# Layer 1's row sums: the product with ones one step later, in the bank of the product with v, and the division another step later

## The chip, the core and the metric

One core of one Trainium2 chip. The metric is the device time of one execution, in microseconds. The kernel before took 2955.73 us, the median of three runs (2946.95 to 2957.67).

## The reference, cut to what matters

Two cross-attention layers follow each other, on x of 4 batches x 1024 rows x 512 and a context of 4 x 1024 x 384, all in float32. Layer 0 has 16 heads of 64. Layer 1, in which the change lies, has 16 heads of 32 and works on layer 0's output:

```python
xn = x * jax.lax.rsqrt(jnp.mean(x * x, axis=-1, keepdims=True) + EPS_RMS) * norm_w
q = (xn @ wq).reshape(B, T_dec, N_HEADS, HEAD_DIM)
kv = (encoder_out @ wkv).reshape(B, T_enc, 2, N_HEADS, HEAD_DIM)
k, v = (kv[:, :, 0], kv[:, :, 1])
q = _rotate(q, cos, sin)
k = _rotate(k, cos, sin)
...
logits = jnp.einsum('bqhd,bkhd->bhqk', q, k) * scale
attn = jax.nn.softmax(logits, axis=-1)
out = jnp.einsum('bhqk,bkhd->bqhd', attn, v).reshape(B, T_dec, D_Q)
return residual + out @ wout
```

The line left out divides each head's q and k by their norms. Since they have norm 1, the exponentials of the logits need no maximum taken off. What the change touches is the division of the softmax: the sum of the exponentials over the keys of each query, and the division of the product with v by it.

## The kernel before, in words

The batches follow each other, and within one layer 0 comes before layer 1. Every engine works through its instructions in the order in which the code records them; nothing reorders them (manual_schedule). What one engine needs of another is a semaphore wait that the tile framework derives from the tiles that an instruction reads and writes.

Layer 1 of a batch is Attention1 (L555). It has two halves of eight heads each, a half has eight blocks, one for each of four query blocks qb (WQ = 256 queries) and each of two head groups g (four heads of 32 rows). A block has four steps, kk = 0 to 3, each of two key blocks of 128 keys, so there are 32 steps in a half, 64 in a batch and 256 in all, and 64 blocks. `step` (L570) records, in this order:

- 8 matmuls of the scores (L577; the profile counts each float32 matmul as two, so 16 there) into two PSUM tiles s of two banks each, and two exponentials from them on ScalarE (L587), into e.
- `finish` (L599): the division that was left over from the step before, if any, and then `product` (L607), the 8 matmuls (L616) of the exponentials of the step before with v, which add up in av[:, 0] over the four steps of a block.
- The filler (L591): `Units.fill` takes off a queue of units as many as their noted costs allow. They are projections (L163), transposes, and output products, with all that hangs on them on the other engines: the rotation of q and k on VectorE (L476 to L483), the norms, the adds of output products to x (L293). In the first half of a batch they make q, k and v of the layer, in the second half output products and the next batch's preparation. In the last half of the last batch there are only output products, which are added to the queue at given steps n (L873 to L876), once the o that they read has been recorded.
- On VectorE, the sum of the two key blocks' exponentials, two adds (L593) into both[:, kk], and in steps 1 and 2 an add of that to both[:, 0] (L597). After a block, both[:, 0] and both[:, 3] together hold the exponentials summed over the eight key blocks.

What is left is the sum over the 128 partitions. `product` does it after the last step of a block (L623): 8 matmuls with a matrix of ones (L627), of both[:, 0] and both[:, 3], into av[:, 1]. These stand right after the last product with v, that is in step 0 of the next block. ScalarE then copies both halves of av to avs (L631), and one step later VectorE takes the reciprocal of the sums in avs (L634) and multiplies (L635) into o.

Each block takes a new av tile, from PSUM's slot f0, which has one buffer; the filler's banks (`bank`, L126) are f1 to f3 during layer 1, and f0 to f3 otherwise. The tile `both` is four slots of 4 x 256 columns.

Of the kernel before, what the change touches and what calls it, by code (L numbers as in the profile page):

```python
# [31 lines left out]
F32 = mybir.dt.float32  # L32
# [4 lines left out]
P = 128  # L37
S = 1024
NT = S // P
# [8 lines left out]
HD1 = 32  # L48
# [60 lines left out]
def xattn_kernel(ctx: ExitStack, tc: tile.TileContext, a: dict, out: bass.AP):  # L109
    nc = tc.nc  # L110
# [6 lines left out]
    ps_f = ctx.enter_context(tc.tile_pool(name="ps_f", bufs=1, space=bass.MemoryType.PSUM))  # L117
    ctx.enter_context(tc.manual_schedule())

    def score(name, shape=(P, S)):  # L120
        return ps_s.tile(list(shape), F32, tag="s", name=name)
# [18 lines left out]
    ones = const.tile([P, HD1], F32, name="ones")  # L140
# [211 lines left out]
    class Attention0:  # L352


        def __init__(self, b, units):
            self.b, self.u = b, units
            self.blocks = deque()
            self.turn = self.raw = None
# [194 lines left out]
    WQ = 256  # L553

    class Attention1:  # L555


        def __init__(self, b, units):
            self.b, self.u = b, units
            self.last = None  # L560
            self.av = None
            self.quotient = None
            self.e = sb.tile([P, 2, 2, 2, 2, WQ], F32, tag="e", bufs=2, name=f"e1_{b}")
            self.both = sb.tile([P, 4, 4, WQ], F32, tag="big", bufs=2, name=f"both_{b}")
            rest = sb.tile([P, 4, 1024], F32, tag="big", bufs=2, name=f"rest_{b}")
            self.avs = rest[:, 0].rearrange("p (n c q) -> p n c q", n=2, c=2)
            v1 = rest[:, 2:].rearrange("p g (t f) -> p g t f", f=P)
            self.v1 = [v1[:, g] for g in range(2)]

        def step(self, half, g, qb, kk, kT, qT, v, o, us):  # L570
            n = f"{self.b}_{half}_{g}_{qb}_{kk}"
            sc = [score(f"s1_{n}_{u}", (P, 2, 2, WQ)) for u in range(2)]
            for c in range(2):
                for j in range(4):
                    rr = slice(j * HD1, (j + 1) * HD1)
                    k = 2 * kk + c
                    nc.tensor.matmul(  # L577
                        sc[j // 2][:, j % 2, c, :],
                        kT[rr, g, k * P : (k + 1) * P],
                        qT[rr, g, qb * WQ : (qb + 1) * WQ],  # L580
                        start=True,
                        stop=True,
                    )
            es = []
            for u in range(2):
                e = self.e[:, kk % 2, u]
                nc.scalar.activation(e, sc[u], AF.Exp, scale=float(np.sqrt(np.float32(HD1))))  # L587
                es.append(e)
            self.finish()
            self.last = (half, g, qb, kk, v, es, o)  # L590
            self.u.fill(us)  # L591
            for u in range(2):
                nc.vector.tensor_add(  # L593
                    self.both[:, kk, 2 * u : 2 * u + 2, :], es[u][:, :, 0, :], es[u][:, :, 1, :]
                )
            if 0 < kk < NT // 2 - 1:
                nc.vector.tensor_add(self.both[:, 0], self.both[:, 0], self.both[:, kk])  # L597

        def finish(self):  # L599

            if self.quotient is not None:
                self.quotient()
                self.quotient = None
            if self.last is not None:
                self.product()

        def product(self):  # L607
            half, g, qb, kk, v, es, o = self.last
            n = f"{self.b}_{half}_{g}_{qb}"
            if kk == 0:  # L610
                self.av = ps_f.tile([P, 2, WQ], F32, tag="f0", name=f"av1_{n}")
            first, end = kk == 0, kk == NT // 2 - 1
            for c in range(2):
                for j in range(4):
                    rr = slice(j * HD1, (j + 1) * HD1)
                    nc.tensor.matmul(  # L616
                        self.av[rr, 0, :],
                        v[g][:, 2 * kk + c, rr],
                        es[j // 2][:, j % 2, c, :],
                        start=first and c == 0,  # L620
                        stop=end and c == 1,
                    )
            if end:  # L623
                for i in (0, NT // 2 - 1):
                    for j in range(4):
                        rr = slice(j * HD1, (j + 1) * HD1)
                        nc.tensor.matmul(  # L627
                            self.av[rr, 1, :], ones, self.both[:, i, j], start=i == 0, stop=i > 0
                        )
                s = self.avs[:, qb % 2]  # L630
                nc.scalar.copy(s, self.av)  # L631

                def divide():
                    nc.vector.reciprocal(s[:, 1, :], s[:, 1, :])  # L634
                    nc.vector.tensor_mul(o[g][:, qb * WQ : (qb + 1) * WQ], s[:, 0, :], s[:, 1, :])  # L635

                self.quotient = divide
            self.last = None


# [5 lines left out]
    def flat(lists):  # L646
        return [u for lst in lists for u in lst]
# [52 lines left out]
    work = Units()  # L700
# [15 lines left out]
    for b in range(B):  # L716
# [7 lines left out]
        for p in range(NPAIR):  # L724
# [8 lines left out]
            elif p % 2 == 0:  # L733
                i = p // 2 - 1
# [4 lines left out]
                    lambda n, i=i: wo[i][:, n % 2, :],  # L739
# [14 lines left out]
            if p == NPAIR - 1:  # L754
# [7 lines left out]
                v = []  # L762
# [10 lines left out]
            n = 7 * (p == 0)  # L773
# [10 lines left out]
            for i in range(NT):  # L784
# [8 lines left out]
                n = NT * (NPAIR - p) - i  # L793
# [27 lines left out]
        att1 = Attention1(b, work)  # L821
        o = [
            sb.tile([P, S], F32, tag="vals", bufs=4, name=f"o1_{b}_{g}") if g < 2 else None
            for g in range(4)
        ]
# [6 lines left out]
        for half in range(2):  # L832
            n = 0
            if half == 0:
                vs = value_chains(att1.v1, wv1, ct, f"pv1_{b}_1")
                first = [q[1], (norms[1]["stats"], [], []), vs[0], (norms[1]["apply"], [], k1[1][2]), k1[2]]
                rest = [(norms[1]["turn"] + q[2][0], [], q[2][2]), k1[3], q[3], q1[0], vs[1], q1[1], q1[2]]
                rest += [q1[3], vs[2], vs[3]]
                chains = first + rest
                work.add(weave(chains, 2))  # L840
                def mark(c):

                    i = chains.index(c)
                    return sum(len(x[0]) for x in chains[: i + 3]) + sum(len(x[2]) for x in chains[: i + 1])

                base = work.done
                marks = {8: base + mark(q[1]), 16: base + mark(rest[0]), 24: base + mark(q[3])}
            else:
                for g in range(2, 4):
                    o[g] = sb.tile([P, S], F32, tag="vals", bufs=4, name=f"o1_{b}_{g}")  # L850
                wo1 = [wo_load(a["wout"], i, f"wo1_{b}_{i}") for i in range(2)]
                adds = add_units(xt, lambda n: o[n], lambda n: wo1[0][:, n % 2, :], f"po1_{b}_0", (0, 1))
                if b + 1 < B:
                    st, order = prepare_units(b + 1)
                    first, later = order(adds)
                    work.add(first)
                else:
                    work.add(flat(adds))
            blocks = [(qb, g) for qb in range(S // WQ) for g in range(2)]
            final = b == B - 1 and half == 1  # L860
            if final:
                blocks.sort(key=lambda block: block[1])
                adds = [
                    add_units(
                        xt, lambda n: o[n], lambda n: wo1[1][:, n % 2, :], f"po1_{b}_{i}", (i,), store if i == 3 else None
                    )
                    for i in (2, 3)
                ]
            for qb, g in blocks:
                for kk in range(NT // 2):  # L870
                    if half == 0 and n in marks:
                        work.until(marks[n])
                    if final and n == 18:  # L873
                        work.add(flat(adds[0]))
                    if final and n in (22, 26, 30):
                        work.add(flat(adds[1][(n - 22) // 2 : (n - 18) // 2]))  # L876
                    att1.step(half, g, qb, kk, kT, qT, v, o[2 * half :], work.total() / (32 - n))
                    n += 1
            work.drain()
            kT, qT, v = kT1, qT1, att1.v1  # L880
        att1.finish()
        att1.quotient()
        which["from"], which["cols"] = 0, 2
        if b == B - 1:
            tail = flat(adds[1][6:])
        else:
            outs = add_units(
                xt, lambda n, o=o: o[n], lambda n, w=wo1[1]: w[:, n % 2, :], f"po1_{b}_1", (2, 3), store
# [40 lines left out]
```

## Time and profile before

| | |
|---|---|
| runs, median (lowest, highest) | 2955.73 us (2946.95, 2957.67) |
| profiled execution: its own time | 2957.42 us |
| profiled execution: span of the instructions | 2955.4 us |
| granted TensorE clock, mean | 0.992 |
| TensorE, VectorE, ScalarE busy | 2865.9, 2185.6, 1436.6 us |
| TensorE idle within a first half of layer 1 | 6.1 us of 128 to 130 us |
| TensorE idle within a second half, batches 0 to 2 | 0.3 us of 123 us |
| L627, product with ones | 1024 in the profile (512 in the code), 81.3 us busy |
| L634, reciprocal | 64, mean 1748 ns |
| L635, multiplication | 64, mean 498 ns |
| L631, copy of av | 64, mean 587 ns |

The page gives busy times by engine, the chain of work that ended last, and groups of instructions with the idle time ahead of them. The answers on waits give, for each pair of instruction and releaser, the idle time in total, how often, and the longest. In the timeline each line is a run of like instructions: start, duration, engine, line, operation, tiles, and in brackets the idle time of the engine ahead of it with what ended it. The rows by window give, after the length, the busy time of PE, PEld, DVE, ACT and POOL with instruction counts, then the granted TensorE clock (PEclk) as a share of full speed, the share of DMA and GB/s. PE is TensorE (PEld its weight loads), DVE VectorE, ACT ScalarE, POOL GpSimd, SP SyncE.

### The profile page before, as it was taken

What the parts mean: (1) busy time and instruction counts of PE and PEld (TensorE: products, weight loads), DVE (VectorE), ACT (ScalarE), POOL (GpSimd) and SP (SyncE); (2) the same over time, 40 slices, a digit from 0 to 9 for tenths busy, and PEclk for the clock granted to TensorE, in tenths of its full rate; (3) what the DMA queues carried; (4) which work ended last, traced back from release to release, by engine and by line L of the source; (5) the groups of instructions that cost most, each with busy time, mean ns of one, the idle gap of its engine ahead of it and who ended that gap; (6) DMA issues with size and microseconds to landing.
All of it is one profiled execution on the core that took longest, in us unless ns stands there. A gap on an engine that the chain in (4) does not pass through costs nothing.

```text
span 2955.4 us, 66614 instructions
## 1 busy us (share of the span) xinstructions
PE 2865.9 (97%) x27336; PEld 1433.0 (48%) x27336; DVE 2185.6 (74%) x2952; ACT 1436.6 (49%) x2265; POOL 935.9 (32%) x776
## 2 busy tenths in 40 slices
PE   8999999999989999999998999999999999999998
PEld 4444445555444454555544444455554444445544
DVE  5677785877767778587776777868877677786787
ACT  4444444656434443466643444346664344444664
POOL 2343353320234335332023433534102343353310
PEclk9999999999999999999999999999999999999999
DMA  5878774010487877401048787730105887763000
GB/s 141 197 180 188 169 173 104 22 36 25 105 199 176 186 163 164 104 22 36 25 115 189 179 187 170 162 94 22 36 25 126 192 182 178 172 162 85 2 2 30
DMA packets 177552, 348.86 MB, mean 118 GB/s; under 512 B 37600, under 2 KB 93152, under 8 KB 177248
## 3 DMA queue, kind: packets, MB, share of 16 engines
q1 hardware_dynamic: 175920, 343.96, 49.5%
q8 instruction: 215, 3.52, 0.5%
q14 instruction: 89, 0.73, 0.1%
q10 hardware_dynamic: 1328, 0.66, 0.1%
HBM read 67.64 MB, written 8.39 MB: 26 GB/s over the span
## 4 chain that ended last, share of the span: by engine, by line
PE 80%; DVE 10%; SPq 4%; DMA 2%; issue 2%; ACT 1%; POOL 1%; DVEq 0%; ACTq 0%
PE s L365 15%; PE av L426 13%; PE po L163 10%; PE s L577 8%; PE pqT L163 7%; PE pv L163 7%; PE av L616 6%; PE pkT L163 6%; SPq L410 4%; PE q_p L163 3%; PE av L627 2%; DVE both L593 2%; DVE m L390 2%; PE k_p L163 1%; DMA wo<-in_Wo_dram 1%
## 5 line engine op out<-in xcount | busy, mean ns | idle before, releaser
L390 DVE TENSOR_REDUCE m<-s 128x1 f32<-128x1024 f32 x512 | 603.0, 1220 | 401.6 <-PE s L365 401.6
L587 ACT ACTIVATE e<-s 128x1024 f32<-128x1024 f32 x512 | 497.1, 1023 | 313.2 <-PE s L577 304.7
L391 ACT ACTIVATE e<-s,m 128x1024 f32<-128x1024 f32 x256 | 283.4, 1112 | 502.9 <-DVE m L390 240.7
L396 POOL TENSOR_SCALAR raw<-raw,li 128x1024 f32<-128x1024 f32 x256 | 286.4, 1119 | 734.2 <-DVE li L395 725.8
L365 PE MATMUL s<-qk 64*128 64x512 f32 x2048 | 518.1, 621 | 0.7 <-ACT qk L135 0.7
L391 ACT ACTIVATE raw<-s,m 128x1024 f32<-128x1024 f32 x256 | 285.9, 1117 | 470.0 <-DVE m L390 470.0
L426 PE MATMUL av<-eT,v 128*64 128x256 f32 x4096 | 470.4, 382 | 5.3 <-DMA eT<-e 2.3
L396 POOL TENSOR_SCALAR e<-e,li 128x1024 f32<-128x1024 f32 x256 | 286.3, 1119 | 493.8 <-DMA eT<-e 239.4
L593 DVE TENSOR_TENSOR both<-e 128x512 f32<-128x512 f32 x512 | 341.9, 701 | 116.1 <-ACT e L587 88.9
L426 PEld LDWEIGHTS av<-eT,v 128*64 128x64 f32 x4096 | 287.4, 137 | 225.2 <-issue 84.5
L365 PEld LDWEIGHTS s<-qk 64*128 64x128 f32 x2048 | 180.9, 188 | 283.9 <-issue 174.3
L577 PE MATMUL s<-q,k 32*128 32x256 f32 x4096 | 306.0, 401 | 5.9 <-ACT q L504 2.7
L399 DVE STREAM_TRANSPOSE e<-e 128x1024 f32<-128x1024 f32 x256 | 310.1, 1229 | 0.2
L399 DVE STREAM_TRANSPOSE e<-raw 128x1024 f32<-128x1024 f32 x256 | 310.0, 1229 | 0.0
L163 PE MATMUL po<-wo,vals 128*64 128x512 f32 x1024 | 242.7, 608 | 26.5 <-DMA wo<-in_Wo_dram 26.5
L577 PEld LDWEIGHTS s<-q,k 32*128 32x128 f32 x4096 | 192.2, 184 | 153.0 <-ACT e L587 72.1
L163 PE MATMUL pqT<-hT,w 128*64 128x512 f32 (+1 forms) x1216 | 240.7, 595 | 2.5 <-ACT hT L247 2.5
L293 DVE TENSOR_TENSOR x<-x,po 128x512 f32<-128x512 f32 x200 | 131.7, 679 | 112.2 <-PE po L163 112.2
L163 PEld LDWEIGHTS pv<-w,cT 128*64 128x64 f32 (+1 forms) x3360 | 170.3, 132 | 41.6 <-issue 34.8
L163 PE MATMUL pv<-w,cT 128*64 128x128 f32 (+1 forms) x3360 | 184.3, 274 | 0.7 <-ACT hT L247 0.7
L163 PE MATMUL pkT<-cT,w 128*64 128x512 f32 (+1 forms) x912 | 183.1, 597 | 0.0
L597 DVE TENSOR_TENSOR both<-both 128x1024 f32<-128x1024 f32 x128 | 159.7, 1248 | 4.4
(81 smaller groups left out, 2793.1 us busy)
## 6 DMA issues: line engine op xcount, KB each, us to landing
eT<-e SPq DMA_DIRECT2D x2048, 128.0 KB, 2.4
xr<-in_x_dram SPq DMA_DIRECT2D x32, 256.0 KB, 3.6
x<-in_x_dram SPq DMA_DIRECT2D x32, 256.0 KB, 4.6
wo<-in_Wo_dram SPq DMA_DIRECT2D x16, 512.0 KB, 4.4
out_dram<-x SPq DMA_DIRECT2D x32, 256.0 KB, 2.6
w<-in_Wq_dram SPq DMA_DIRECT2D x31, 256.0 KB, 3.1
c<-in_ctx_dram SPq DMA_DIRECT2D x32, 192.0 KB, 3.9
wkv<-in_wkv_dram SPq DMA_DIRECT2D x16, 384.0 KB, 3.4
```

Of the source, the lines that this page charges most:

```text
L163: nc.tensor.matmul(o[rr], lhsT[:, rr], rhs, start=start, stop=stop)
L365: nc.tensor.matmul(sc[j][:, kb * 512 : (kb + 1) * 512], pr["qT"][r[j], i * P : (i + 1) * P], pr["kT"][r[j], kb * 512 : (kb + 1) * 512], st ...
L390: nc.vector.tensor_reduce(m[:, j : j + 1], sc[j], AX.X, ALU.max, negate=True)
L391: nc.scalar.activation(e[j], sc[j].rearrange("p (g s) -> p g s", g=4), AF.Exp, bias=m[:, j : j + 1], accum_out=l[:, j : j + 1])
L396: nc.gpsimd.tensor_scalar(e[j], e[j], li[:, j : j + 1], HD0**-0.5, ALU.mult, ALU.mult)
L399: self.turn = [lambda j=j: nc.vector.transpose(self.e[:, :, i % BQ * 2 + j, :], e[j]) for j in range(2)]
L426: nc.tensor.matmul(av[r[j], :W].rearrange("p (t a i) -> p t a i", t=BQ, a=4), pr["v"][:, k, r[j]], eT[:, j, :, :, k * 32 : (k + 1) * 32], ...
L577: nc.tensor.matmul(sc[j // 2][:, j % 2, c, :], kT[rr, g, k * P : (k + 1) * P], qT[rr, g, qb * WQ : (qb + 1) * WQ], start=True, stop=True,)
L587: nc.scalar.activation(e, sc[u], AF.Exp, scale=float(np.sqrt(np.float32(HD1))))
L593: nc.vector.tensor_add(self.both[:, kk, 2 * u : 2 * u + 2, :], es[u][:, :, 0, :], es[u][:, :, 1, :])
L597: nc.vector.tensor_add(self.both[:, 0], self.both[:, 0], self.both[:, kk])
L616: nc.tensor.matmul(self.av[rr, 0, :], v[g][:, 2 * kk + c, rr], es[j // 2][:, j % 2, c, :], start=first and c == 0, stop=end and c == 1,)
```

## The change

- av is one tile for all blocks of a batch, made when Attention1 is. The product with v uses columns 0 of it, the product with ones columns 1.
- `product` no longer records the product with ones; after the last step of a block it records the copy of av[:, 0] alone (L625 after) and leaves `sums` over.
- `finish` calls what was left over ahead of the product: `sums`, the product with ones (L631 after), comes in step 1 of the next block between its scores and the product of step 0, and leaves `divide` over, which comes in step 2, ahead of the product of step 1. Its reciprocal (L634 after) reads the sums in av[:, 1] in PSUM, and writes to avs.
- The first sum of a block, and what steps 1 and 2 add to it, is in both[:, 0] or both[:, 1] by turns; steps 1 and 2 use both[:, 2] for their own sums, step 3 both[:, 3] as before.
- At the end of a batch `finish` is called three times. In the last half of the last batch, output products that read o join the queue one step later.

```diff
         def __init__(self, b, units):
-            self.av = None
-            self.quotient = None
+            self.av = ps_f.tile([P, 2, WQ], F32, tag="f0", name=f"av1_{b}")
+            self.after = None
+            self.n = 0
...
         def step(self, half, g, qb, kk, kT, qT, v, o, us):
+            self.n += kk == 0
...
             self.finish()
-            self.last = (half, g, qb, kk, v, es, o)
+            self.last = (half, g, qb, kk, v, es, o, self.n % 2)
             self.u.fill(us)
+
+            acc, end = self.both[:, self.n % 2], self.both[:, 3]
+            into = acc if kk == 0 else end if kk == NT // 2 - 1 else self.both[:, 2]
             for u in range(2):
-                nc.vector.tensor_add(
-                    self.both[:, kk, 2 * u : 2 * u + 2, :], es[u][:, :, 0, :], es[u][:, :, 1, :]
-                )
+                nc.vector.tensor_add(into[:, 2 * u : 2 * u + 2, :], es[u][:, :, 0, :], es[u][:, :, 1, :])
             if 0 < kk < NT // 2 - 1:
-                nc.vector.tensor_add(self.both[:, 0], self.both[:, 0], self.both[:, kk])
+                nc.vector.tensor_add(acc, acc, into)

         def finish(self):
-            if self.quotient is not None:
-                self.quotient()
-                self.quotient = None
+            if self.after is not None:
+                self.after = self.after()
             if self.last is not None:
                 self.product()

         def product(self):
-            half, g, qb, kk, v, es, o = self.last
+            half, g, qb, kk, v, es, o, par = self.last
-            if kk == 0:
-                self.av = ps_f.tile([P, 2, WQ], F32, tag="f0", name=f"av1_{n}")
...
             if end:
-                for i in (0, NT // 2 - 1):
-                    for j in range(4):
-                        rr = slice(j * HD1, (j + 1) * HD1)
-                        nc.tensor.matmul(
-                            self.av[rr, 1, :], ones, self.both[:, i, j], start=i == 0, stop=i > 0
-                        )
-                s = self.avs[:, qb % 2]
-                nc.scalar.copy(s, self.av)
-
-                def divide():
-                    nc.vector.reciprocal(s[:, 1, :], s[:, 1, :])
-                    nc.vector.tensor_mul(o[g][:, qb * WQ : (qb + 1) * WQ], s[:, 0, :], s[:, 1, :])
-
-                self.quotient = divide
+                s = self.avs[:, par]
+                nc.scalar.copy(s[:, 0, :], self.av[:, 0, :])
+
+                def sums():
+                    for i in (par, 3):
+                        for j in range(4):
+                            rr = slice(j * HD1, (j + 1) * HD1)
+                            nc.tensor.matmul(self.av[rr, 1, :], ones, self.both[:, i, j], start=i != 3, stop=i == 3)
+
+                    def divide():
+                        nc.vector.reciprocal(s[:, 1, :], self.av[:, 1, :])
+                        nc.vector.tensor_mul(o[g][:, qb * WQ : (qb + 1) * WQ], s[:, 0, :], s[:, 1, :])
+
+                    return divide
+
+                self.after = sums
             self.last = None
...
-                    if final and n in (22, 26, 30):
-                        work.add(flat(adds[1][(n - 22) // 2 : (n - 18) // 2]))
+                    if final and n in (23, 27, 31):
+                        work.add(flat(adds[1][(n - 23) // 2 : (n - 19) // 2]))
...
-        att1.finish()
-        att1.quotient()
+        for _ in range(3):
+            att1.finish()
```

## The prediction

> **What bounds the kernel now.** I read the page first, then the waits, then the timeline of layer 1. In what follows a block is one (qb, g) of layer 1: four steps, kk = 0 to 3, of two key blocks of 128. A batch has two halves of eight blocks.
>
> ```profile
> PE 2865.9 (97%) x27336; PEld 1433.0 (48%) x27336; DVE 2185.6 (74%) x2952; ACT 1436.6 (49%) x2265; POOL 935.9 (32%) x776
> ...
> PEclk9999999999999999999999999999999999999999
> ```
>
> TensorE is busy for 97% of the span and 90 us are idle in all, so an idle microsecond of TensorE in layer 1 is a microsecond of the span, and no edit here removes matmuls. The waits name what the change can touch:
>
> ```profile
> DVE both L593 <- PE av L627: 26.8, 10, 2.9
> ...
> PE av L627 <- DVE both L593: 15.4, 9, 2.2
> ```
>
> The second row (us in total, times, longest): TensorE sat idle for 15.4 us ahead of products with ones (L627) because the last sum of the exponentials (L593) was late. The first is VectorE waiting to overwrite what those products still read; VectorE is not the bound, so it costs little by itself.
>
> The timeline of a plain second step (kk = 1, second half of batch 1) shows the chain that matters after the change:
>
> ```profile
> 1461.61 1.75 DVE L634 RECIPROCAL rest<-rest 128x256 f32<-128x256 f32 x1
> ...
> 1462.39 1.15 PE L577 MATMUL s<-q,k 32*128 32x256 f32 x16
> 1463.39 0.42 DVE L635 TENSOR_TENSOR o<-rest 128x256 f32<-128x256 f32 x1
> ...
> 1463.46 1.07 PE L616 MATMUL av<-e,rest 128*32 128x256 f32 x16
> 1463.57 1.94 ACT L587 ACTIVATE e<-s 128x1024 f32<-128x1024 f32 x2 [2.17 <-PE s L577]
> ...
> 1464.35 1.04 PE L163 MATMUL pkT<-cT,w 128*32 128x512 f32 x8
> 1464.62 0.69 DVE L593 TENSOR_TENSOR both<-e 128x512 f32<-128x512 f32 x1 [0.81 <-ACT e L587]
> ...
> 1465.32 1.37 PE L577 MATMUL s<-q,k 32*128 32x256 f32 x16
> ...
> 1465.54 0.69 DVE L593 TENSOR_TENSOR both<-e 128x512 f32<-128x512 f32 x1 [0.23 <-ACT e L587]
> 1466.27 1.23 DVE L597 TENSOR_TENSOR both<-both 128x1024 f32<-128x1024 f32 x1
> ...
> 1466.62 1.07 PE L616 MATMUL av<-e,rest 128*32 128x256 f32 x16
> ```
>
> TensorE goes scores, product of the step before, filler (L163), next scores, product of kk = 1 at 1466.62. The division (L634, L635) was over at 1463.8, ahead of this step's sums; L597 ends at 1467.50.
>
> [...] The changed program does order by bank: in its instruction order, 60 of the 64 products of kk = 1 (L616) wait for VectorE's reciprocal (L634 after), though one writes av[:,0] and the other reads av[:,1]. [...]
>
> ```profile
> 609.70:612.00 2.30, 0.07 (x6) 0.02 (x2) 2.27 (x5) 0.60 (x1) 0.58 (x1) 1.00 0.00 0
> 612.40:615.80 3.40, 3.40 (x30) 1.35 (x28) 2.84 (x4) 0.59 (x1) 3.32 (x2) 0.50 0.00 0
> ...
> 2599.10:2601.90 2.80, 0.07 (x4) 0.05 (x2) 2.80 (x6) 1.51 (x3) 2.63 (x3) 1.00 0.00 0
> 2602.40:2605.80 3.40, 3.40 (x12) 1.32 (x10) 0.00 (x0) 0.00 (x0) 0.96 (x1) 0.50 0.95 212
> ```
>
> The PEclk column reads 0.50 after idle stretches of 2.2 and 2.7 us. Every idle stretch of 2.4 us or more in this trace was followed by half clock, of four of 2.23 us one, of eight of 1.56 to 1.67 us none. [...] The trace shows no reciprocal from PSUM; its add with a PSUM operand (L293) took 679 ns against 701 for L593. I take nothing[...].
>
> **The change part by part.**
>
> *Ones one step later.* The same 8 matmuls (16 in the profile), 1.05 us, so no work goes. In each first half five of their groups last 3.40, 1.83, 1.46, 1.23 and 4.06 us in the timeline instead of 1.05: 6.7 us too long. One step later the sums are long there. Gain 4 x 6.7 = 27 us. (The 15.4 us of the waits are the part shown as idle.)
>
> *First sums in two places.* VectorE's 26.8 us of waiting go. It gets ahead by that, off TensorE's path: nothing.
>
> *Copy of half the bank.* 64 copies fall from 587 to about 373 ns (the 128x256 copy of L135). ScalarE is 49% busy; nothing. The ones now wait for this copy, issued a step earlier and done by then: nothing; if it were late, the cost is at most its 0.37 us.
>
> *The division from the bank, another step later.* It no longer waits for the copy; at the very end that takes 0.6 us off (L631's 0.59 stands between ones and reciprocal). But in VectorE's queue it moves behind the sums and the add of kk = 1, and the product of kk = 1 waits for it. Behind the waiting matmul on TensorE lie its filler and the scores of kk = 3; then ScalarE and VectorE wait for those. Its reads also wait for the product of kk = 0, long done. It issues no DMA; output fillers of the last half go from steps 22, 26, 30 to 23, 27, 31, their stores behind them, and SP and POOL see no other order.
>
> The price in the plain step: ones no longer stand ahead of the scores, so exponentials end 0.87 us earlier (a group of ones delays the next by 0.87), at 1464.64 instead of 1465.51. Then 1.98 to the end of L597, as now, 1.75 for the reciprocal, 0.06 to be seen: 1468.43. TensorE's product stood at 1466.62, so 1.8 us are lost. The filler between product and scores, 1.0 us here, is what would hide it; 3.0 us would be needed. Where a rotation lies in VectorE's queue in that step it is worse:
>
> ```profile
> 1273.68 0.69 DVE L478 TENSOR_TENSOR rot<-q_p,cos 128x512 f32<-128x512 f32 x1 [2.29 <-ACT rot L476]
> ...
> 1276.27 1.28 DVE L593 TENSOR_TENSOR both<-e 128x512 f32<-128x512 f32 x2
> 1277.59 1.23 DVE L597 TENSOR_TENSOR both<-both 128x1024 f32<-128x1024 f32 x1
> ```
>
> The rotation starts from a projection that doesn't move, L597 ends at 1278.81, the reciprocal at 1280.6; the product stood at 1273.99: 6.6 us. I did this for each boundary from its own rows. First half (seven): 2.5, 6.6, 1.5, 5.8, 1.6, 3.6, 1.5 = 23.1. Second half of batches 0 to 2 (eight): 0.6, 3.8, 1.1, 1.6, 3.3, 1.2, 1.8, 1.8 = 15.2; 3.8 and 3.3 have an output add (L293) ahead of the sums. Last half: five of 1.8, three of 3.8 = 20.4. Sum 4 x 23.1 + 3 x 15.2 + 20.4 = 158. If the reciprocal ended 1.75 us after today's L597 everywhere, it would be 220; if the whole 2.17 us of division were saved ahead of L597, 90.
>
> *Clock.* Idle of over 2.4 us comes three times in a first half (12), twice in a second half (6), eight times in the last (there the scores, which today wait for ScalarE, stop doing so, so TensorE idles 2.8 us for a loss of 1.8), and at half of the four first boundaries (2): 28. One drop costs 1.6 us: batch 0's first half, the only one with a drop, took 129.7 us, the others 128.1. 28 x 1.6 - 1.6 = 43 us. Bounds: 0, and 90 if all but the shortest stalls drop it.
>
> Sum: 158 - 27 - 1 + 43 = +173 on the profiled execution's 2957.4 us (span 2955.4): 3131. That execution lies 1.7 us above the median, so 3130.
>
> **The rivals.** *The clock stays up:* the same stalls without the drops, 3087. For it: [...]only one of four of 2.23 us did it. Against: all of 2.4 and more did. *Short stalls:* VectorE gets ahead by the waits it loses and the division is mostly done early: the low sum, 90 - 27 = +63, 3019. Against: in plain steps ScalarE, not VectorE, ends last, and rotations hang on projections. *Faster:* the bank is free when the product comes; then the ones' waits go and nothing returns, -28 us, 2928. It decides by the reciprocal's end against the start of the product of kk = 1: filler in the second step would have to be 3.0 us, and only the first block of a second half (2.5) comes near.
>
> **How the numbers follow.** Stalls with drops (3090 to 3180): 0.62. Stalls at full clock (3050 to 3090): 0.2. Short stalls (2975 to 3050): 0.1. Faster: 0.05; about no change, stalls just eating the 28 us: 0.03. A difference under 0.5%, 15 us, is not told from none here. The range leaves out faster, no change, most of short stalls and a few per cent above: 3055 to 3185.
>
> **What would show it.** Right: a row of L616 waiting for the reciprocal, about 158 us over some 60 waits, longest near 7; no wait of the ones for sums; PEclk at half in more places in layer 1; first halves about 16 + 5 us longer, second ones 15 + 4, layer 0 unchanged. Wrong: few or short waits of L616 for VectorE, or idle ahead of the ones again.

## The result, and the profile after

The changed kernel took 3131.32 us, the median of four runs (3125.22 to 3135.44), against 2951.94 us for the kernel before in the same measurement (2946.95 to 2957.67). The ratio is 1.0605, with a 95% interval of 1.0576 to 1.0635: 6% slower. The profiled execution took 3125.22 us, with a span of 3123.4 us, 168 us more than before. The forecast was 3130 us.

The page after, its rows of busy time and of the granted clock:

```profile
PE 2895.0 (93%) x27336; PEld 1441.2 (46%) x27336; DVE 2192.1 (70%) x2952; ACT 1419.9 (45%) x2265; POOL 929.9 (30%) x776
...
PEclk9999999999999999999999999999999999999998
```

The same 27336 matmuls keep TensorE busy for 29 us longer than before, and its share of the span falls from 97% to 93%. So TensorE both waits more and works more slowly. The row of PEclk hardly shows the second: a slice is 78 us long, and the 3.4 to 10.2 us of most stretches at half clock in this run don't move a rounded tenth. Short windows, below, show it.

What TensorE waited for, after (us in total, times, longest):

```profile
PE av L616 <- DVE rest L634: 154.9, 60, 6.5
PE po L163 <- DMA wo<-in_Wo_dram: 24.9, 6, 9.5
```

The first row is new. It is the product of step 1 waiting for VectorE's reciprocal, in 60 of 64 blocks, as the order of instructions had it. The wait of the ones for the sums, 15.4 us before, has no row any more. The sum closes: 155 us of new waiting, less 15 of old, and 29 us of longer busy time make 169 us, against 168 measured.

The timeline of the plain step that the prediction worked through (second half of batch 1), now:

```profile
1539.88 1.15 PE L579 MATMUL s<-q,k 32*128 32x256 f32 x16
...
1540.96 1.07 PE L631 MATMUL av<-both,ones 128*32 128x256 f32 x16
1541.06 1.94 ACT L589 ACTIVATE e<-s 128x1024 f32<-128x1024 f32 x2 [1.59 <-PE s L579]
...
1541.85 1.05 PE L616 MATMUL av<-e,rest 128*32 128x256 f32 x16
...
1543.77 1.23 DVE L600 TENSOR_TENSOR both<-both 128x1024 f32<-128x1024 f32 x1
...
1544.91 1.75 DVE L634 RECIPROCAL rest<-av 128x256 f32<-128x256 f32 x1
1546.69 0.43 DVE L635 TENSOR_TENSOR o<-rest 128x256 f32<-128x256 f32 x1
...
1546.71 1.07 PE L616 MATMUL av<-e,rest 128*32 128x256 f32 x16 [1.89 <-DVE rest L634]
```

The reciprocal stands behind step 1's sums and add (L600), ends at 1546.66, and TensorE's next product starts 0.05 us later. From the start of the scores that is 6.83 us; the prediction had 6.91 (1461.52, which is 1462.39 less 0.87, to 1468.43). Where a rotation (L478 to L483) lies ahead of these sums in VectorE's queue, in two blocks of each first half, the waits are 6.48 and 5.33 us. The first of them in batch 1:

```profile
1317.53 0.69 DVE L478 TENSOR_TENSOR rot<-q_p,cos 128x512 f32<-128x512 f32 x1 [4.48 <-ACT rot L476]
...
1322.58 1.75 DVE L634 RECIPROCAL rest<-av 128x256 f32<-128x256 f32 x1
...
1324.39 1.08 PE L616 MATMUL av<-e,v 128*32 128x256 f32 x8 [6.48 <-DVE rest L634]
```

### The profile page after: what moved, and what is told of

It is laid out like the page before. It is cut to its first block, busy times and chain, and to the rows that moved or that the text cites. A ratio compares the mean times of both kernels' runs of the same rounds, so it can differ in the third digit from the quotient of the medians.

```text
span 3123.4 us, 66582 instructions
## 1 busy us (share of the span) xinstructions
PE 2895.0 (93%) x27336; PEld 1441.2 (46%) x27336; DVE 2192.1 (70%) x2952; ACT 1419.9 (45%) x2265; POOL 929.9 (30%) x776
## 4 chain that ended last, share of the span: by engine, by line
PE 74%; DVE 15%; SPq 4%; issue 3%; ACT 2%; DMA 2%; POOL 1%; DVEq 0%; ACTq 0%
PE s L365 14%; PE av L426 12%; PE po L163 9%; PE av L616 6%; PE pv L163 6%; PE pqT L163 6%; PE s L579 6%; PE pkT L163 5%; SPq L410 4%; DVE rest L634 3%; PE q_p L163 3%; DVE both L600 2%; DVE both L598 2%; PE k_p L163 2%; DVE m L390 2%
## 5 line engine op out<-in xcount | busy, mean ns | idle before, releaser
L598 DVE TENSOR_TENSOR both<-e 128x512 f32<-128x512 f32 x512 | 340.6, 694 | 187.4 <-ACT e L589 187.1
L293 DVE TENSOR_TENSOR x<-x,po 128x512 f32<-128x512 f32 x200 | 132.4, 679 | 152.6 <-PE po L163 152.6
L616 PE MATMUL av<-e,v 128*32 128x256 f32 x2048 | 144.1, 401 | 88.5 <-DVE rest L634 88.5
L616 PE MATMUL av<-e,rest 128*32 128x256 f32 x2048 | 141.5, 395 | 66.4 <-DVE rest L634 66.4
```

Source lines behind the costliest of these rows:

```text
L293: nc.vector.tensor_add(xt[t], xt[t], pp[0])
L598: nc.vector.tensor_add(into[:, 2 * u : 2 * u + 2, :], es[u][:, :, 0, :], es[u][:, :, 1, :])
L616: nc.tensor.matmul(self.av[rr, 0, :], v[g][:, 2 * kk + c, rr], es[j // 2][:, j % 2, c, :], start=first and c == 0, stop=end and c == 1,)
```

## The experiments

The experiments have numbers, the theories letters, as in the expectations that stand before each result.

**Experiment 1: the division's place in VectorE's queue.** Theory A was that the loss is a chain: the exponentials on ScalarE, then sums, add and reciprocal in VectorE's order, with TensorE at its end because the bank is shared. Rivals were that sharing a bank costs wherever the division stands (B), and that moving the ones costs by itself (C). Only the place of the division was changed:

```diff
         def finish(self):
-            if self.after is not None:
-                self.after = self.after()
+            then, self.after = self.after, None
+            if then is not None:
+                then = then()
             if self.last is not None:
                 self.product()
+            if then is not None:
+                then()
...
-        for _ in range(3):
+        for _ in range(2):
             att1.finish()
```

> The changed kernel, with the division recorded in step 1 of the next block, right behind the product of step 0, instead of a step later behind step 1's sums. The bank stays shared and the product of step 1 still waits for the reciprocal. Theory A (the loss is VectorE's place in the queue: exponentials, sums, add and rotation stand ahead of a reciprocal that TensorE waits for): the reciprocal ends about when the product comes; TensorE's wait for it falls from 155 us to under 15, the gain from the ones' waits stays, about 2930 us. Theory B (sharing one bank costs by itself, wherever the division stands): still over 3050 us. Theory C (the ones one step later cost by themselves): still over 3050 us, with the wait at the ones.

Measured: 2930.11 us, ratio to before 0.9912 (0.9897 to 0.9927). TensorE's waits in this run:

```profile
PE k_p L163 <- DVE x L293: 8.2, 3, 2.7
PE av L619 <- DVE rest L637: 7.4, 9, 1.0
```

155 us became 7.4. Theory A stands, and the two rivals fall with one edit: the bank is still shared, and the ones still come a step later. The timeline of the same plain step shows how closely it fits:

```profile
1452.06 1.05 PE L619 MATMUL av<-e,rest 128*32 128x256 f32 x16
...
1453.24 1.76 DVE L637 RECIPROCAL rest<-av 128x256 f32<-128x256 f32 x1 [3.09 <-ACT e L589]
...
1455.05 1.07 PE L619 MATMUL av<-e,rest 128*32 128x256 f32 x16
```

The reciprocal now starts when the product of step 0 is through, ahead of the sums, and ends at 1455.00; the next product starts at 1455.05, 4.96 us after its scores (1450.09) instead of 6.83. The bracket names ScalarE for VectorE's idle time, though the exponentials aren't read here. The profile infers the releaser, and names the last of several, so the order of the code has to be read beside it.

**Experiment 2: let ScalarE free the bank.** ScalarE copies the sums out behind the product of step 0; the reciprocal stays a step later and reads the copy.

```diff
         def finish(self):
+            copy = None
             if self.after is not None:
                 self.after = self.after()
+                copy = self.after and self.after[0]
             if self.last is not None:
                 self.product()
+            if copy:
+                copy()
+                self.after = self.after[1]
...
-                        nc.vector.reciprocal(s[:, 1, :], self.av[:, 1, :])
+                        nc.vector.reciprocal(s[:, 1, :], s[:, 1, :])
...
-                    return divide
+                    return (lambda: nc.scalar.copy(s[:, 1, :], self.av[:, 1, :])), divide
```

> The changed kernel, with the sums copied by ScalarE out of the bank behind the product of step 0 (64 copies more, about 0.37 us each), and the reciprocal a step later from that copy, as before the change. The bank stays shared, but TensorE's product of step 1 now waits for the copy, not for VectorE. Theory A: the copy ends 0.4 us behind the exponentials, ahead of the product; the stall goes, about 2930 us. Theory B (one bank for both costs by itself) and theory C (ones a step later cost): over 3050 us.

Measured: 2938.53 us, ratio 0.994 (0.9925 to 0.9955). That is 17 us less than before, though 8 us above what was expected. No row of TensorE waiting for a reciprocal is left. So the shared bank costs little as soon as the engine that reads it is done early; that holds for VectorE in experiment 1, with 7.4 us of waiting left, and for ScalarE here. The 8 us were not pinned down. Compared with experiment 1, TensorE waits 5.2 us again for sums ahead of the ones, and 29.8 us instead of 19.2 for the DMA of wo.

**Experiment 3: twice the suspected cost.**

```diff
                         nc.vector.reciprocal(s[:, 1, :], self.av[:, 1, :])
+                        nc.vector.reciprocal(s[:, 1, :], self.av[:, 1, :])
```

> The changed kernel with the reciprocal of the sums taken twice (the second writes the same values over the first). Theory A: TensorE waits for the later one, so each of 60 stalls grows by 1.75 us, 105 us, and some more clock drops, 10 to 45 us: 3240 to 3285 us. If the wait were satisfied by something else, or VectorE had room there: within 20 us of the changed kernel's 3131.

Measured: 3299.95 us, ratio to before 1.1165 (1.1148 to 1.1182), above the range given.

```profile
PE av L616 <- DVE rest L635: 262.2, 60, 8.3
```

The wait grew by 107 us, 60 times 1.79, which is what was expected of it. The rest was underrated, with 10 to 45 us expected: TensorE's busy time grew by another 64 us (2959.3 against 2895.0). The clock record has 66 stretches at half speed, 329 us in all, against 29 and 160 us in the changed kernel and 9 and 52 us before.

**Experiment 4: the first sums in two places alone**, put into the kernel before.

```diff
+            acc, end = self.both[:, self.n % 2], self.both[:, 3]
+            into = acc if kk == 0 else end if kk == NT // 2 - 1 else self.both[:, 2]
...
-                for i in (0, NT // 2 - 1):
+                for i in (par, 3):
```

> The kernel before with only the first sums in two places by turns. Theory A: VectorE's 26.8 us of waiting for the ones go, but they are off TensorE's path; TensorE's 15.4 us ahead of the ones stay nearly whole: within 10 us of before. Rival: the sums come earlier because VectorE no longer waits, and the 15.4 us go too: 2930 us.

Measured: 2957.15 us, ratio 1.0008 (0.9998 to 1.0018): no difference. TensorE's wait ahead of the ones is still there:

```profile
PE av L629 <- DVE both L597: 16.9, 9, 2.4
```

So the gain in experiments 1 and 2 doesn't come from the two places alone; by elimination it comes from the ones standing a step later, which needs the two places. VectorE's own 26.8 us of waiting are gone in this run, and were worth nothing, as costed.

**Experiment 5: a bank for the sums, and its price.** The sums get f1, and the filler keeps two banks in layer 1. Beside it the kernel before with two filler banks, and the sums' own bank together with the early division of experiment 1.

```diff
+            self.sum = ps_f.tile([P, WQ], F32, tag="f1", name=f"sum1_{b}")
...
-                            nc.tensor.matmul(self.av[rr, 1, :], ones, self.both[:, i, j], start=i != 3, stop=i == 3)
+                            nc.tensor.matmul(self.sum[rr], ones, self.both[:, i, j], start=i != 3, stop=i == 3)
...
-                        nc.vector.reciprocal(s[:, 1, :], self.av[:, 1, :])
+                        nc.vector.reciprocal(s[:, 1, :], self.sum)
...
-        which["from"], which["cols"] = 1, 4
+        which["from"], which["cols"] = 2, 4
+        which["n"] = max(which["n"], 1)
```

> The changed kernel with the sums in a bank of their own (f1), the division where the change put it; the filler is left with two banks (f2, f3) in layer 1. No product with v waits for VectorE's reciprocal any more. Theory A (the wait exists only because the two share a bank): the 155 us of waiting go, and with them the clock drops: 2925 us plus whatever two filler banks cost, which the next run measures. Theory D (the order alone, division behind step 1's sums, costs, with or without the bank): over 3050 us.

> The kernel before with two filler banks in layer 1 instead of three: the price of the bank that the run with a bank for the sums takes from the filler. Expected 0 to 60 us over before, from short waits of the filler's first matmuls for ScalarE's or VectorE's readers of the bank.

> Sums in a bank of their own and the division in step 1 right behind the product of step 0. Theory A: nothing more than one of the two repairs alone, since either takes the stall away: within 10 us of the run with the sums' own bank. If the 7 us that TensorE still waits for the reciprocal in the run with the early division alone matter, this run is up to 7 us better than that one, less the price of two filler banks.

Measured, with ratios to before (2953.39 us): the sums' own bank 2985.62 us, 1.0119 (1.0101 to 1.0136); before with two filler banks 2989.08 us, 1.0123 (1.0105 to 1.014); own bank and early division 2967.75 us, 1.0053 (1.0037 to 1.0068).

The own bank removes the wait for the reciprocal, with the division where the change put it: 146 of the 178 us lost against this measurement's before go, although the filler loses a bank. So the wait is due to what the two share, and theory D, that the order costs over 100 us by itself, falls. What they share is one tile in one bank; the own bank is another tile too, and no run parts the bank from the tile as the cause. And the bank costs the filler 36 us, more than the 25 us that experiment 1 wins.

With the early division the parts add up: experiment 1's 2930 us and 36 make 2966, and 2968 was measured. With the late one they don't: the 2925 that was expected and 36 would be 2961, and 2986 was measured. 18 us of these 25 come back with the early division, which was expected to matter by less than 10. So the late division costs something even in a bank of its own. With two filler banks the filler waits for VectorE's rotation to be done with a bank. A division ahead of the rotation in VectorE's queue could make that later, but this is not shown. The own bank with the late division:

```profile
PE q_p L163 <- DVE rot L480: 17.9, 8, 2.5
PE pv L163 <- DVE rot L480: 14.3, 8, 2.0
```

and with the early one:

```profile
PE pv L163 <- DVE rot L480: 19.2, 8, 3.2
...
PE q_p L163 <- DVE rot L480: 7.9, 4, 2.0
```

These two rows make 5 us of the 14.8 by which the profiled executions differ (2983.8 and 2969.0). Waits for adds of output products (L293) make 6 more, and TensorE's busy time 5 (2866.7 and 2861.4); smaller waits go the other way.

**Experiment 6: output products at the old steps**, on top of experiment 1.

```diff
-                    if final and n in (23, 27, 31):
-                        work.add(flat(adds[1][(n - 23) // 2 : (n - 19) // 2]))
+                    if final and n in (22, 26, 30):
+                        work.add(flat(adds[1][(n - 22) // 2 : (n - 18) // 2]))
```

> The kernel with the division in step 1 behind the product of step 0, and the output products of the last half joining the queue at steps 22, 26 and 30 as before the change, since o is there a step earlier again. Theory A: the last half is 1 to 3 us shorter or the same: 2926 to 2931 us.

Measured: 2933.7 us (2927.6 to 2938.18), ratio 0.9937 (0.9921 to 0.9953): just above the range expected and not to be told from the 2930.11 of experiment 1. The last half, from its first to its last scores, went from 103.8 us to 104.7 us in the profiles, so the hoped-for gain isn't there. Experiment 1 is the version to keep.

## Why the prediction was right, point by point

*The mechanism* was read off the instruction order and priced from the timeline, and held: 60 waits, the longest 6.5 us where 6.6 was worked out. That the product with v has to stand behind a reader of the other columns is the program's order. The runs show its price, 154.9 us; whether the hardware needs it was not shown.

*The stalls* were put at 158 us of lost time, which with the idle times of 2.8 us given for the last half makes 163 us of idle time; 154.9 us was measured. By boundary, in order, the first half of batch 1, and within 0.01 us those of the others, shows 1.45, 6.48, 1.88, 5.33, 1.45, 3.47 and 2.07 us where the prediction had 2.5, 6.6, 1.5, 5.8, 1.6, 3.6 and 1.5. The second half of batch 1 has under 0.3, 3.87, 0.90, 1.43, 3.01, 0.80, 1.88 and 1.88 where it had 0.6, 3.8, 1.1, 1.6, 3.3, 1.2, 1.8 and 1.8. In the last half it is 2.5 and 3.9 us where losses of 1.8 and 3.8 and idle times of 2.8 had been given. The first boundary was wrong by a microsecond, the others by less. From the first scores of a half to those of the next, first halves are 20.5 to 24.0 us longer than before, where 21 had been given. From first to last scores, second halves of batches 0 to 2 are 15.9 to 19.8 longer, where 19 had been given. The last half is 26.8 longer, less than the 33 that its stalls and eight drops of 1.6 make.

*The gain* was put at 27 us for the ones and 1 at the end. Experiment 1, which has it with 7.4 us of stalls left, is 25 us below before. In batches 1 to 3 its first halves take 125.5 us against 130.5, with 1.0 us of stall in each, so 6.0 us a half where 6.7 had been given.

*The clock* was put at 28 drops of 1.6 us, 45 us, or 43 without the one that was there before. The changed kernel has 23 drops in layer 1, fewer, but several last 6.8 or 10.2 us instead of 3.4. What they cost is best read from experiment 1, which has the same matmuls without the stalls: the spans differ by 194.7 us (3123.4 and 2928.7), idle waits for the reciprocal by 147.5, and TensorE's busy time by 47.2 (2895.0 and 2847.8). Against the kernel before, busy time is only 29 us longer, because there some 12 us of the ones' lateness (27 less the 15.4 shown as idle) stood in it. By that estimate 41 us compare with the 43 of the forecast. So the mechanism was right, but that the sum came so near is in part luck: the count was too high and the length too short. That it is mostly the clock and not another slowness shows in two halves of the changed kernel with the same work and the same stalls, the second halves of batches 1 and 2 (windows; the columns are explained at the profile before). The third line is the second half of batch 1 in experiment 1:

```profile
1429.30:1566.60 137.30, 123.02 (x1709) 62.42 (x1708) 91.72 (x127) 76.69 (x95) 3.07 (x4) 0.99 0.10 32
2200.10:2341.30 141.20, 126.91 (x1705) 63.89 (x1704) 91.69 (x127) 76.82 (x95) 3.07 (x4) 0.95 0.11 32
...
1351.70:1473.10 121.40, 121.14 (x1709) 62.42 (x1708) 88.02 (x124) 76.67 (x95) 3.07 (x4) 1.00 0.12 36
```

The mean clock is 0.99 in the first and 0.95 in the second; the clock record has 3.4 us at half speed in one and 13.6 in the other. The 3.9 us that the second half is longer are all in TensorE's busy time (126.91 and 123.02), 0.38 us for each microsecond at half clock. The changed kernel has 160.5 us at half clock and experiment 1 35.0; for these 125.5 us more, 0.38 gives an estimate of 48 us, next to the 47.2. Experiment 3 has 64 us more busy time than the changed kernel for 168 us more at half clock, again 0.38. The figure is a mean over stretches that lie in part within a stall: of 120 us at half clock in layer 1 of the changed kernel, TensorE was busy for 94. Nor is all of it the clock. The second half of batch 1 is busy for 1.9 us more than its like in experiment 1 (123.02 and 121.14), and of that its 3.4 us at half clock explain 1.3 at 0.38, or 1.7 at one half. Over eight halves that leaves, by estimate, 1 to 5 us of the 47 open. The clock itself was not varied by an experiment; this is a comparison of traces.

*The rivals.* Without clock drops it would have been 3087: the drops were there, and 3131 less 47 is 3084. The short stalls (3019) would have needed VectorE to get ahead; in plain steps ScalarE's exponentials ended last, and VectorE sat idle for them for 187.1 us in all ahead of the sums (L598). The faster case failed at the point that the prediction gave, the filler in the second step against 3.0 us: the three waits under 0.3 us are those of the first blocks of the second halves of batches 0 to 2, where the filler is 2.5 us. The two together make 2.8, by estimate the filler that would have been enough.

*When half clock came.* In the changed kernel half clock followed two of the ten stalls of 1.88 us and one of the four of 3.47 us, and set in during or after each of the 14 of 3.87 us or more. Between about 1.9 and 3.5 us, then, it was open here whether a stall brought half clock. That the prediction took every idle time over 2.4 us for a drop was too sharp, and its own trace has an exception that it overlooked: 2.46 us of idle time near the start of the kernel before, with the clock full behind it:

```profile
35.00:37.46 2.46, 0.01 (x2) 0.00 (x1) 2.46 (x4) 2.46 (x6) 0.68 (x1) 1.00 0.00 0
37.50:40.90 3.40, 3.40 (x16) 1.20 (x18) 0.38 (x2) 1.92 (x3) 1.52 (x2) 1.00 0.02 5
```

## What to carry to other kernels

Before an accumulator and its reader are put into one PSUM bank to save a copy, ask who touches that bank next and what stands in the reader's queue ahead of the read: with the reciprocal recorded right behind the last write the kernel was 0.9% faster than before, with it one step later 6% slower. A copy that looks like waste may be what frees the bank early: with one of the sums (experiment 2) the kernel took 2938.53 us, against 3131.32 without. Where TensorE stalls again and again, look at the clock too: here 60 stalls of 2.6 us in the mean came with 23 stretches at half clock in layer 1, and the clock was by estimate about a quarter of the loss (47 of the 195 us between the changed kernel and experiment 1).

## What the runs showed of the hardware that was not expected

- The reciprocal of 128 x 256 float32 took 1750 ns from PSUM (changed kernel) and 1748 ns from SBUF (kernel before), means of 64 each: the PSUM source shows no cost here.
- Stretches at half clock in the changed kernel lasted 3.4, 6.8 or 10.2 us, apart from one that runs to its end. None of the eight stalls of 1.45 us was followed by one; all four of 6.48 us had one that began before the stall was over.
